# An attention layer and two quantized convolutions on one core: reading eleven images back in three pieces, and another order of products in the first two heads

## The chip, the core and the metric

The kernel runs on one core of one Trainium2 chip. A core has a matrix engine (TensorE, here PE), which multiplies a stationary operand, loaded first (PEld), by a moving one and writes to PSUM; a vector engine (DVE), a scalar engine (ACT), GpSimd (POOL) and a queue engine (SP) for DMAs. SBUF is the working memory of 128 partitions, PSUM the memory of eight banks that PE writes to. Each engine works through its own instructions in order and waits for semaphores of others. The metric is the device time of one execution in microseconds (us); lower is better.

## What is computed

The input is 16 images of 128 channels and 32 x 32 points (N = 1024). Layer 0 is attention over the points with four heads and a residual; layer 1 is two 3 x 3 convolutions on quantized activations and weights, each followed by a batch norm over all images, and a residual.

```python
qkv = einsum('bchw,oc->bohw', x, w_qkv) + b_qkv          # four heads of q, k, v
scores = einsum('bnc,bcm->bnm', q, k) * c ** -0.5
out = einsum('bnm,bmc->bnc', softmax(scores), v)
x = einsum('bchw,oc->bohw', out, w_out) + b_out + x

out = conv3x3(act_quant(x), weight_quant(w1))             # act_quant: 16 levels of [0, 1]
out = conv3x3(act_quant(batchnorm(out)), weight_quant(w2))
return batchnorm(out) + x
```

The batch norm between the convolutions needs the mean and variance of all 16 images, so the second convolution can't start before the first is done for every image.

## The kernel before

**The attention.** The weights are folded first. `fold_a(h)` makes `at_sb`, the product of the query and key weights of head h, and its bias `au_sb`; `fold_b` makes `bt_sb`, the product of value and output weights. For head number g = 4b + h (image b), `project_u(g, hf)` (L500) makes half hf of `u`, 512 of the 1024 queries: a product of `at_sb` and the image, copied out of PSUM with its bias by DVE for the very first half and by ACT otherwise. `scores(g, k)` (L545) is a step: four PSUM tiles `pss` of 128 keys x 512 queries, each followed by an exponential on ACT into one slot of `e`. A tile (c, m) has the keys of chunk k + 4c and the query half m, so it reads half m of `u` alone; the order of the four is (0, 1), (1, 1), (0, 0), (1, 0) in every step. The slots are named B12, B22, B11 and B21 in that order. DVE then combines them: T3 = B12 + B22 (L556), T1 and T2 (L557), T4 (L560). The next step's `attend` does seven half-width products of `e` and `vo` into the four banks `psa` instead of eight. A DMA of SP or GpSimd (L566, L568) adds the exponentials up for the softmax's denominator. `project_v` (L522) makes `vo` from the image and `bt_sb`, in two parts c = 0 and 1.

All of PE's products of this stage pass `product` (L402), which holds them to the order in which the program calls them. That order is written by hand: the loop at L961 runs the steps, `at(step, half, fn, ...)` puts other work behind a step's scores (half 0) or behind its `attend` (half 1), and `between` puts a call behind one tile of scores. In step 1 `between` puts the two parts of the first `project_v` behind tiles 0 and 1. The other engines' instructions are ordered by a scheduler when the program is built.

**The start.** `warm_up(3)` (L442) issues three products of a block of ones that nobody reads, into a PSUM tile of `ps_a`, while the first weights and the first image are loaded. Then come `fold_a(0)`, and both halves of `project_u(0)`, then step 0. The second head's `u` is made by `project_u(1, 0)` at (2, 1) and `project_u(1, 1)` at (3, 1) (L957, L958), the latter as the last thing before the scores of head 1. `u` and `psv` outside of the first steps share the single bank of `ps_m`.

**The first convolution** runs beside the attention, image by image. Its outputs `ys[b]` of images 4 to 14 (`AWAY`) are written to `y1d` in main memory, since SBUF is full; those of 0 to 3 and 15 stay.

**The second stage** (from L1010) reuses the SBUF of the attention. SP issues one DMA (L1046) that brings all eleven images back into `back`, and then the residual `x1` of all images (L1051). `quantize2(b)` (L1053) scales image b on ACT (L1061), clamps it on DVE (L1062) and writes it to a padded buffer, on DVE up to image 5 (L1066) and on ACT after (L1068). Six images (`FILTERED`: 3, 5, 7, 9, 11, 13) are convolved with fewer products from sums of rows, `rows` (L1077), two on DVE and two on GpSimd, and put together from the PSUM tiles `psf` by ACT (L1097) and DVE (L1098 to L1101); the others are convolved directly, `psc` (L282), and copied out by ACT (L293). DVE takes the statistics of each (L298). The loop at L1110 quantizes one image ahead: behind the convolution of image 0 image 2, of 1 image 5, of 2 image 4, of 3 image 7, of 4 image 6 and so on. Images 0 to 3 need nothing read back. When all statistics are there, each image is scaled, the residual added, and stored (L1129).

Of the kernel before, what the change touches and what calls it, by code (L numbers as in the profile page):

```python
# [9 lines left out]
F32 = mybir.dt.float32  # L10
# [183 lines left out]
def fast_path(  # L194
# [17 lines left out]
    P = 128  # L212
    B, C, N = x.shape
# [16 lines left out]
    ones = sums[:, 0 : 2 * P // (N // Q), :].rearrange("p g k -> p (g k)")  # L230
# [11 lines left out]
    AWAY = range(4, B - 1)  # L242
# [131 lines left out]
    with ExitStack() as ph:  # L374
# [27 lines left out]
        def product(out_, lhsT, rhs, start=True, stop=True):  # L402

            with tc.issue_after(pe[0]) if pe else nullcontext():
                done = nc.tensor.matmul(out_, lhsT=lhsT, rhs=rhs, start=start, stop=stop)  # L405
            pe[:] = [done.ins]
            return done
# [32 lines left out]
                nc.scalar.dma_start(out=bnp_sb, in_=bnp)  # L440

        def warm_up(n):  # L442


            ps = ps_a.tile([P, 2 * P], F32, tag="a0", name="unread")
            for _ in range(n):
                product(ps, ones[:, 0:P], ones)


        at_sb = once.tile([P, NH, P], F32, name="at_sb")  # L450
# [49 lines left out]
        def project_u(g, hf, ps=None):  # L500
            b, h = heads[g]
            if hf == 0:
                us[g] = up.tile([P, N], F32, tag="u", name=f"u_{g}")
            if ps is None:
                ps = ps_m.tile([P, HALF], F32, tag="mm", name=f"psu_{g}_{hf}")
            halves(ps, lambda t: at_sb[:, h, LANES[t]], xt[b][:, ts(hf, HALF)])
            dst = us[g][:, ts(hf, HALF)]
            if g == 0 and hf == 0:
                nc.vector.tensor_scalar(dst, ps, au_sb[:, h : h + 1], None, ALU.add)
            else:  # L510
                copied = nc.scalar.activation(dst, ps, AF.Identity, bias=au_sb[:, h : h + 1])  # L511
                if g == 0:
                    load_rest(copied.ins)
# [31 lines left out]
        def scores(g, k, between=None):  # L545


            b, h = heads[g]
            e = es[g, k] = ep.tile([P, 7, HALF], F32, tag="e", name=f"e_{g}_{k}")
            for i, (c, m) in enumerate(((0, 1), (1, 1), (0, 0), (1, 0))):  # L550
                ps = ps_s.tile([P, HALF], F32, tag="s", name=f"pss_{g}_{k}_{i}")
                score(ps, b, g, k + NK * c, ts(m, HALF))
                exps[:] = [nc.scalar.activation(e[:, 2 * c + 1 - m], ps, AF.Exp).ins]  # L553
                if between and i in between:
                    between[i]()
            nc.vector.tensor_tensor(e[:, T3], e[:, B12], e[:, B22], ALU.add)  # L556
            nc.vector.tensor_tensor(  # L557
                e[:, T1 : T2 + 1 : T2 - T1], e[:, B12 : B11 + 1], e[:, B11 : T3 + 1 : T3 - B11], ALU.subtract
            )
            last = nc.vector.tensor_tensor(e[:, T4], e[:, T2], e[:, B21], ALU.add)  # L560
            combined[g, k] = last.ins
            mine = e[:, T4 : T3 + 1]
            sums_added[:] = [last.ins]
            if k == 0:
                sides[g] = esp.tile([P, NHF, HALF], F32, tag="es", name=f"es_{g}")
                nc.sync.dma_start(out=sides[g], in_=mine)  # L566
            else:
                nc.gpsimd.dma_start(out=sides[g], in_=mine, accum_op=ALU.add)  # L568
# [336 lines left out]
        def at(step, half, fn, *args):  # L905

            later.setdefault(2 * step + half, []).append((fn, args))

        def run(step, half):
            for fn, args in later.pop(2 * step + half, ()):  # L910
                fn(*args)

        warm_up(3)
        fold_a(0)
        for hf in range(NHF):
            ps = ps_a.tile([P, HALF], F32, tag=f"a{2 + hf}", name=f"psu_0_{hf}")
            project_u(0, hf, ps)
        at(1, 0, load_second)
# [36 lines left out]
                for i, (step, half) in enumerate(when):  # L955
                    at(g * NK + step, half, project_v, b + 1, *divmod(i, 2))
        at(2, 1, project_u, 1, 0)  # L957
        at(3, 1, project_u, 1, 1)  # L958
        at(n_steps, 1, gather, 0)

        for step in range(n_steps):  # L961
            g, k = divmod(step, NK)
            between = {}
            if step == 1:
                banks = [ps_a.tile([P, HALF], F32, tag=f"a{2 + c}", name=f"psv_0_{c}") for c in range(2)]
                between = {0: lambda: project_v(0, 0, 0, banks[0]), 1: lambda: project_v(0, 0, 1, banks[1])}
            scores(g, k, between)
            if step == 0:
                fold_b()
            elif step < NK:  # L970
                project_v(0, step, 0)
            run(step, 0)
            if step > 0:
                attend(*divmod(step - 1, NK))
            if 0 < step < NK:
                ps = ps_s.tile([P, HALF], F32, tag="s", name=f"psv_0_{step}_1")
                project_v(0, step, 1, ps)
            run(step, 1)
# [31 lines left out]
    with ExitStack() as ph:  # L1010
# [31 lines left out]


        scale1, bias1 = bn_params(0)
        back = resp.tile([P, len(AWAY), N], F32, name="back")
        nc.sync.dma_start(out=back, in_=y1d.rearrange("b c n -> c b n"))  # L1046
        for i, b in enumerate(AWAY):
            ys[b] = back[:, i]
        x1 = resp.tile([P, B, N], F32, name="res")
        for some in (slice(0, B - 1), slice(B - 1, B)):  # L1050
            nc.sync.dma_start(out=x1[:, some], in_=x1d[some].rearrange("b c n -> c b n"))  # L1051
# [360 lines left out]
```

## Time and profile before

| | |
|---|---|
| time, median of 3 runs | 2020.92 us (2020.81 to 2023.84) |
| the profiled execution | 2020.84 us, of which 2018.7 us are the span of the trace |
| granted PE clock, mean | 0.992 |
| longest groups: `pss` matmuls | 1032.5 us, 4128 of them |
| `psa` matmuls | 922.4 us, 3624 of them |
| exponentials on ACT (L553) | 594.9 us, 1008 of them, 595 ns each |
| second convolution, first and last matmul | 1927.64 to 1987.3 us |
| memory traffic while the images are read back | 410 to 420 GB/s, 1921 to 1957 us |

The span is the time from the first to the last instruction; 2.1 us lie around it. A line of a group or a wait names the engine, what is written and the line of the kernel: "PE pss L405 <- ACT u L511" is PE waiting, before a product into `pss`, for ACT to write `u`. All products of the attention have line 405, that of the recording helper, so they are told apart by the tile. Matmuls overlap in the pipeline: a product of 512 columns of one pass is listed with some 590 ns and the next starts 430 ns later. PE is busy in nearly the whole span, so the places that matter are the few where it waits.

### The profile page before, as it was taken

The numbers are of one execution on the slowest core, as the hardware profiler recorded it, in microseconds if no ns is written. First come the engines' busy times: TensorE is split into PE (matmuls) and PEld (weight loads), VectorE is DVE, ScalarE is ACT, GpSimd is POOL, SyncE is SP. The second block draws the span as 40 slices with busy tenths as digits, with TensorE's granted clock in tenths as the row PEclk, the third lists the DMA queues.
The fourth block names the chain that finished last, engine by engine and source line by source line (L and its number), as shares of the span: only waits on it lengthen the run. The fifth ranks groups of instructions, "written<-read, shape, count | busy, mean of one in ns | idle before, by whom it ended". The sixth has DMA issues, their size and how long they took to land.

```text
span 2018.7 us, 25810 instructions
## 1 busy us (share of the span) xinstructions
PE 1980.5 (98%) x9676; PEld 864.9 (43%) x9677; DVE 1539.8 (76%) x2564; ACT 1185.8 (59%) x1992; POOL 187.5 (9%) x218
## 2 busy tenths in 40 slices
PE   9999999999999999999999999999999999999993
PEld 3444444444434444444444444444444444444541
DVE  3878787776878777687777868877786877778797
ACT  4565665565566566556556556655655665665575
POOL 1101000000100000010010000001001000000021
PEclk9999999999999999999999999999999999999997
DMA  3334333333433433333333333333343334324174
GB/s 85 88 71 94 74 94 73 84 74 74 94 73 84 94 75 92 75 85 83 94 84 76 92 73 94 83 94 76 71 105 74 90 78 94 84 63 97 40 292 168
DMA packets 50501, 181.19 MB, mean 90 GB/s; under 512 B 5568, under 2 KB 5952, under 8 KB 50368
## 3 DMA queue, kind: packets, MB, share of 16 engines
q0 software_dynamic: 27216, 99.10, 25.9%
q1 hardware_dynamic: 19952, 70.33, 8.9%
q10 hardware_dynamic: 3200, 10.03, 1.6%
q8 instruction: 77, 1.26, 0.3%
q14 instruction: 56, 0.46, 0.1%
HBM read 24.78 MB, written 22.54 MB: 23 GB/s over the span
## 4 chain that ended last, share of the span: by engine, by line
PE 97%; DVE 1%; issue 1%; ACT 0%; POOL 0%; DMA 0%; SPq 0%; DVEq 0%; POOLq 0%; ACTq 0%
PE pss L405 43%; PE psa L405 37%; PE psu L405 5%; PE psv L405 5%; PE psc L282 2%; PE psw L405 2%; PE psf L1086 1%; DVE back L1139 0%; POOL worst L371 0%; DVE y L1139 0%; DMA x<-in_x_dram 0%; DVE e L557 0%; ACT y L1136 0%; DVE steps L1062 0%; ACT e L553 0%
## 5 line engine op out<-in xcount | busy, mean ns | idle before, releaser
L405 PE MATMUL pss<-u,x 128*64 128x512 f32 (+1 forms) x4128 | 1032.5, 589 | 1.9 <-ACT u L511 1.6
L405 PE MATMUL psa<-e,vo 128*64 128x512 f32 (+1 forms) x3624 | 922.4, 588 | 0.0
L553 ACT ACTIVATE e<-pss 128x512 f32<-128x512 f32 x1008 | 594.9, 595 | 370.5 <-PE pss L405 366.6
L405 PEld LDWEIGHTS pss<-u,x 128*64 128x64 f32 x4128 | 391.5, 137 | 502.6 <-issue 451.2
L405 PEld LDWEIGHTS psa<-e,vo 128*64 128x64 f32 x3624 | 350.7, 137 | 428.4 <-issue 401.3
L556 DVE TENSOR_TENSOR e<-e 128x512 f32<-128x512 f32 x252 | 172.1, 683 | 352.1 <-ACT e L553 352.1
L557 DVE TENSOR_TENSOR e<-e 128x1024 f32<-128x1024 f32 x252 | 308.4, 1224 | 31.0 <-ACT e L553 20.9
L568 POOL DMA_DIRECT2D es<-e x189 | 163.0, 863 | 1688.2 <-DVE e L560 1642.8
L560 DVE TENSOR_TENSOR e<-e 128x512 f32<-128x512 f32 x252 | 174.1, 691 | 21.0
L598 ACT COPY ev<-psa 128x512 f32<-128x512 f32 x252 | 135.4, 589 | 90.2 <-PE psa L405 90.2
L405 PE MATMUL psv<-bt_sb,x 128*64 128x512 f32 x512 | 184.9, 592 | 1.0 <-ACT bt_sb L482 1.0
L405 PE MATMUL psu<-x,at_sb 128*64 128x512 f32 x512 | 184.3, 597 | 0.3 <-DMA x<-in_x_dram 0.3
L532 ACT COPY vo<-psv 128x512 f32<-128x512 f32 x128 | 75.5, 590 | 142.1 <-PE psv L405 142.1
L511 ACT ACTIVATE u<-psu,au_sb 128x512 f32<-128x512 f32 x127 | 87.3, 688 | 16.5 <-PE psu L405 14.8
L405 PEld LDWEIGHTS psv<-bt_sb,x 128*64 128x64 f32 x512 | 57.8, 137 | 65.1 <-issue 59.5
L405 PEld LDWEIGHTS psu<-x,at_sb 128*64 128x64 f32 x512 | 58.1, 138 | 63.0 <-issue 61.2
L628 DVE TRANSPOSE_TENSOR_REDUCE part<-es 128x32 f32<-128x1024 f32 (+1 forms) x65 | 79.4, 1221 | 5.9 <-DMA es<-e 5.9
L668 DVE STREAM_TRANSPOSE rb<-sums 128x1024 f32<-128x1024 f32 (+1 forms) x66 | 79.9, 1211 | 2.1
L838 ACT COPY m<-psw 128x512 f32<-128x512 f32 x45 | 26.3, 585 | 92.5 <-PE psw L405 91.4
L679 DVE TENSOR_TENSOR av<-av,rb 128x1024 f32<-128x1024 f32 x47 | 57.6, 1225 | 1.6
L680 DVE TENSOR_TENSOR acc<-acc,av 128x1024 f32<-128x1024 f32 x47 | 57.5, 1224 | 1.5
L618 ACT COPY ev<-y 64x512 f32<-64x512 f32 x63 | 38.8, 615 | 30.5 <-DVE y L616 28.6
(164 smaller groups left out, 1188.8 us busy)
## 6 DMA issues: line engine op xcount, KB each, us to landing
es<-e POOLq DMA_DIRECT2D x189, 512.0 KB, 4.5
es<-e SPq DMA_DIRECT2D x63, 512.0 KB, 2.9
x_dram<-acc SPq DMA_DIRECT2D x16, 512.0 KB, 4.4
x<-in_x_dram ACTq DMA_DIRECT2D x15, 512.0 KB, 4.7
res<-x_dram SPq DMA_DIRECT2D x1, 7680.0 KB, 35.8
y_dram<-y SPq DMA_DIRECT2D x11, 512.0 KB, 2.6
back<-y_dram SPq DMA_DIRECT2D x1, 5632.0 KB, 18.0
out_dram<-back SPq DMA_DIRECT2D x10, 512.0 KB, 3.0
```

The lines of the kernel that those rows point to most:

```text
L405: done = nc.tensor.matmul(out_, lhsT=lhsT, rhs=rhs, start=start, stop=stop)
L511: copied = nc.scalar.activation(dst, ps, AF.Identity, bias=au_sb[:, h : h + 1])
L532: nc.scalar.copy(v[:, c : c + 3 : 2], ps.rearrange("p (h a o) -> p a h o", a=2, o=PH))
L553: exps[:] = [nc.scalar.activation(e[:, 2 * c + 1 - m], ps, AF.Exp).ins]
L556: nc.vector.tensor_tensor(e[:, T3], e[:, B12], e[:, B22], ALU.add)
L557: nc.vector.tensor_tensor(e[:, T1 : T2 + 1 : T2 - T1], e[:, B12 : B11 + 1], e[:, B11 : T3 + 1 : T3 - B11], ALU.subtract)
L560: last = nc.vector.tensor_tensor(e[:, T4], e[:, T2], e[:, B21], ALU.add)
L568: nc.gpsimd.dma_start(out=sides[g], in_=mine, accum_op=ALU.add)
L598: nc.scalar.copy(to, ps)
L628: nc.vector.tensor_reduce(part, total.rearrange("p (k c) -> p k c", c=Q), AX.X, ALU.add, apply_transpose=True,)
L668: nc.vector.transpose(rb, rinv.unsqueeze(2).to_broadcast([P, n, Q]))
L679: nc.vector.tensor_tensor(av, av, rb, ALU.mult)
```

## The change

Four things are changed.

- `warm_up` writes to one tile `unread`, made once before, and one more unread product is issued before each half of `project_u(0)`.
- In the first step of the first head the tiles of query half 0 come first: (0, 0), (1, 0), (0, 1), (1, 1). All other steps stay as they are.
- In step 1 the two parts of `project_v` stand behind tiles 1 and 2 instead of 0 and 1. The second half of head 1's `u`, `project_u(1, 1)`, stands behind tile 1 of step 3's scores instead of behind that step's `attend` and the products after it.
- The eleven images come back in three DMAs into three tiles: images 4 and 5, images 6 to 8, images 9 to 14. Their sizes are 1024, 1536 and 3072 KB.

With these, the scheduler puts some instructions of ACT, DVE and SP in another order. On SP the store of the last image's residual (L762), which stood behind the single read, stands behind the first of the three. On ACT the quantizings of images 5, 4, 7 and 6 stand before copies of the second convolution's images 0 to 2 that they stood behind. On DVE, at the start, the copy of L481 stands before L560 instead of behind it.

```diff
--- before.py
+++ after.py
@@ -440,11 +440,8 @@
                 nc.scalar.dma_start(out=bnp_sb, in_=bnp)
 
         def warm_up(n):
-
-
-            ps = ps_a.tile([P, 2 * P], F32, tag="a0", name="unread")
             for _ in range(n):
-                product(ps, ones[:, 0:P], ones)
+                product(unread, ones[:, 0:P], ones)
 
 
         at_sb = once.tile([P, NH, P], F32, name="at_sb")
@@ -547,7 +544,8 @@
 
             b, h = heads[g]
             e = es[g, k] = ep.tile([P, 7, HALF], F32, tag="e", name=f"e_{g}_{k}")
-            for i, (c, m) in enumerate(((0, 1), (1, 1), (0, 0), (1, 0))):
+            tiles = ((0, 1), (1, 1), (0, 0), (1, 0))
+            for i, (c, m) in enumerate(tiles[2:] + tiles[:2] if (g, k) == (0, 0) else tiles):
                 ps = ps_s.tile([P, HALF], F32, tag="s", name=f"pss_{g}_{k}_{i}")
                 score(ps, b, g, k + NK * c, ts(m, HALF))
                 exps[:] = [nc.scalar.activation(e[:, 2 * c + 1 - m], ps, AF.Exp).ins]
@@ -910,9 +908,11 @@
             for fn, args in later.pop(2 * step + half, ()):
                 fn(*args)
 
+        unread = ps_a.tile([P, 2 * P], F32, tag="a0", name="unread")
         warm_up(3)
         fold_a(0)
         for hf in range(NHF):
+            warm_up(1)
             ps = ps_a.tile([P, HALF], F32, tag=f"a{2 + hf}", name=f"psu_0_{hf}")
             project_u(0, hf, ps)
         at(1, 0, load_second)
@@ -955,7 +955,6 @@
                 for i, (step, half) in enumerate(when):
                     at(g * NK + step, half, project_v, b + 1, *divmod(i, 2))
         at(2, 1, project_u, 1, 0)
-        at(3, 1, project_u, 1, 1)
         at(n_steps, 1, gather, 0)
 
         for step in range(n_steps):
@@ -963,7 +962,9 @@
             between = {}
             if step == 1:
                 banks = [ps_a.tile([P, HALF], F32, tag=f"a{2 + c}", name=f"psv_0_{c}") for c in range(2)]
-                between = {0: lambda: project_v(0, 0, 0, banks[0]), 1: lambda: project_v(0, 0, 1, banks[1])}
+                between = {1: lambda: project_v(0, 0, 0, banks[0]), 2: lambda: project_v(0, 0, 1, banks[1])}
+            elif step == NK - 1:
+                between = {1: lambda: project_u(1, 1)}
             scores(g, k, between)
             if step == 0:
                 fold_b()
@@ -1042,10 +1043,11 @@
 
 
         scale1, bias1 = bn_params(0)
-        back = resp.tile([P, len(AWAY), N], F32, name="back")
-        nc.sync.dma_start(out=back, in_=y1d.rearrange("b c n -> c b n"))
-        for i, b in enumerate(AWAY):
-            ys[b] = back[:, i]
+        for lo, hi in ((0, 2), (2, 5), (5, len(AWAY))):
+            back = resp.tile([P, hi - lo, N], F32, name=f"back{lo}")
+            nc.sync.dma_start(out=back, in_=y1d[lo:hi].rearrange("b c n -> c b n"))
+            for i in range(lo, hi):
+                ys[AWAY.start + i] = back[:, i - lo]
         x1 = resp.tile([P, B, N], F32, name="res")
         for some in (slice(0, B - 1), slice(B - 1, B)):
             nc.sync.dma_start(out=x1[:, some], in_=x1d[some].rearrange("b c n -> c b n"))
```

## The prediction

> **What bounds the kernel now.** I read the whole span first (busy time, then the chain that ended last), then what the matrix engine (PE) waited for, then the stretches where it waited.
>
> ```profile
> PE 1980.5 (98%) x9676; PEld 864.9 (43%) x9677; DVE 1539.8 (76%) x2564; ACT 1185.8 (59%) x1992; POOL 187.5 (9%) x218
> ...
> PE 97%; DVE 1%; issue 1%; ACT 0%; POOL 0%; DMA 0%; SPq 0%; DVEq 0%; POOLq 0%; ACTq 0%
> ```
>
> The reader sees that only time taken from PE, or a PE stall removed, can shorten the span. PE's waits, over the whole span:
>
> ```profile
> PE psc L282 <- DVE pad L1066: 2.5, 2, 2.1
> PE pss L405 <- ACT u L511: 1.6, 2, 0.8
> PE unread L405 <- POOL sums L231: 1.1, 1, 1.1
> PE psv L405 <- ACT bt_sb L482: 1.0, 1, 1.0
> PE psu L405 <- DMA x<-in_x_dram: 0.3, 1, 0.3
> PE pss L405 <- ACT e L553: 0.3, 1, 0.3
> ```
>
> (us in total, times, longest.) That is all: 6.8 us, in the first 46 us and once near 1943. The timeline of the start places the small ones:
>
> ```profile
> 5.01 2.95 PE L405 MATMUL psu<-x,at_sb 128*64 128x512 f32 x8 [0.35 <-DMA x<-in_x_dram]
> ...
> 8.74 3.65 PE L405 MATMUL pss<-u,x 128*64 128x512 f32 x16 [0.78 <-ACT u L511]
> ...
> 15.53 1.08 PE L405 MATMUL psv<-bt_sb,x 128*64 128x512 f32 x4 [1.04 <-ACT bt_sb L482]
> ...
> 45.41 3.65 PE L405 MATMUL pss<-u,x 128*64 128x512 f32 x16 [0.79 <-ACT u L511]
> ```
>
> The chain of waits around the big one (start, us, what), and then the busy time of the engines there (columns: us, busy and count of PE, PEld, DVE, ACT, POOL, then granted clock, DMA share, GB/s):
>
> ```profile
> 1938.32 1.25 ACT steps L1061
> ...
> 1940.52 1.73 DVE rows L1077 x2
> 1942.24 1.27 DVE steps L1062
> ...
> 1944.51 5.79 PE psc L282 x18
> ...
> 1952.94 3.97 PE psc L282 x18
> ```
>
> ```profile
> 1938.00:1944.00 6.00, 4.37 (x20) 1.75 (x18) 5.03 (x7) 5.91 (x7) 2.67 (x2) 1.00 1.03 419
> 1944.00:1950.00 6.00, 5.49 (x18) 2.17 (x19) 6.00 (x11) 3.76 (x4) 2.48 (x2) 0.72 1.03 410
> 1950.00:1956.00 6.00, 6.00 (x29) 2.65 (x28) 5.99 (x12) 5.68 (x8) 1.03 (x1) 1.00 1.02 409
> ```
>
> Image 4 comes back from memory, ACT can first quantize from it at 1938.32, and PE's convolution of image 4 starts at 1944.51 after 2.14 us idle. Its 18 matmuls then take 5.79 us where the next 18 take 3.97: the clock share is 0.72 in that stretch. So one late read costs 2.14 + (5.79 - 3.97) = about 3.9 us. From 1944 on DVE is busy 6.00 and 5.99 of 6 us, so it is nearly as tight as PE.
>
> ```profile
> back<-y_dram SPq DMA_DIRECT2D x1, 5632.0 KB, 18.0
> ```
>
> ```profile
> L1077 DVE TENSOR_TENSOR rows<-padf x12: 428/1074/1367, 1931.5 to 1970.6; 128x544 bf16<-128x544 bf16 x12
> ```
>
> The read of 5632 KB lands after 18.0 us, at 1937.3; ACT's first use is 1 us later.
>
> **What the Trainium skill says.** "TensorE: Matmul & The Clock Gate", section "What's actually happening": PE falls to half clock after an idle window of 3413 ns, the window runs freely. The trace agrees with the length: (1 - 0.72) x 6 us = 1.7 us lost, so 3.4 us at half; here 2.1 us idle were enough. "DMA: Bandwidth & Descriptors", "Queues, rings and completion order": descriptors are consumed in ring order. The trace agrees: the 512 KB store of the last image, issued behind the big read, needs 17.1 us to land (median of such stores 4.4), so a small first piece will land early. "SBUF — State Buffer", "SBUF: two separate sides": DVE operations with two SBUF inputs or in a two-port mode and GpSimd operations exclude each other. It agrees: the same subtraction on DVE takes 428 to 1367 ns, the long ones beside GpSimd's.
>
> **The change part by part.**
>
> *Part A, the start.* Two unread products are added, one before each half of `psu`. At the half clock of this point one costs two passes of 0.43 us (passes start at 1.68, 2.10, 2.53 in the trace). The first starts at about 4.45, when the bias product is issued; it fills the 0.35 us idle and pushes `psu` 0 from 5.01 to about 5.30. `psu` 0 takes 2 x 0.87, the second unread product goes in at 7.04, by then at full clock (passes of 0.21): `psu` 1 at 7.49, done issuing at 8.35. The scores no longer wait for ACT's second half of `u`: the two tiles put first read only the half that DVE wrote (0.75 us, here 7.26 to 8.01). So scores start at 8.35 instead of 8.74: 0.39 us gained. But all four exponentials now come before DVE's first combination, since B12 and B22 are last: the last exponential ends at 12.65, then 0.69 (L556) and 1.23 (L557) on DVE, ready 14.65. The scheduler puts the copy L481 before L560 in exchange, so it ends at 14.85; L560, 0.69, and the subtraction L483, 0.43, at 15.80. `psv` waits for it and for ACT's L482, which now stands behind a second exponential: that one starts at 15.00 (13.88 for its scores plus the 1.12 us that exp follows them by), L482 at 15.49 plus 0.45. `psv` starts at 16.0. It started at 15.53 with one tile of scores (0.86 us) still to do; that tile is now done before it. So 15.53 + 0.86 - 16.0 = 0.4 us gained, and PE's idle before it grows from 1.04 to about 1.25. Bounds: -0.2 if the cold clock lasts over both unread products (then 1.7 us of them, less the idle they fill and the 1.2 us no longer waited), +0.8 if `psv` comes earlier than I work out.
>
> *Part B, head 1.* `psu` 1 moves from 43.54, right ahead of the scores that wait for it, to between the second and third tile of step 3 (near 36.0). The 0.79 us wait at 45.41 goes. What is late next: the bank of `psu` 0, which ACT frees at 36.03, so at most 0.06 us there; the next user of that bank (`psv` of step 3) comes 1.7 us after `psu` 1, ACT's copy ends 0.95 us after it at the latest. Gain 0.75, bounds 0.5 to 0.8.
>
> *Part C, the reading back.* One DMA becomes three of 1024, 1536 and 3072 KB: two more issues on SP (0.38 us each, nobody waits for SP there). The first keeps all waits of the single one, the last of which is the end of the attention matmuls at 1919.2, so nothing starts earlier. The store of the last image is next in SP's queue, then the other two pieces. At 412 GB/s from 1921: the first piece lands near 1924, the second (3.15 MB in all) near 1929 to 1931, the third where the store landed before, 1938.6. ACT's order is changed with it: image 5 is quantized behind image 2, at 1931.6, image 4 at 1933.2, images 7 and 6 at 1934.8, and the third piece is first wanted near 1943. No read is waited for. Image 4 is in its padded buffer at about 1940.1: DVE's `rows` of image 5 beside GpSimd's to 1938.3, then 0.41, 0.68, 0.41 and 0.43. PE wants it at 1942.4. So the 2.14 us and the 1.8 us of slow clock go: 3.9 as the upper bound. But DVE becomes the limit. It was idle only 0.46 + 1.34 + 0.45 us before 1944, and 0.7 in small steps from 1960. Following DVE in its new order with the durations of the trace, it waits about 1.7 us for ACT near 1941 to 1944 (ACT now does five 1.2 us quantizings ahead of the copies of image 2), and is then only about 1 us ahead of before; from there to the end it saves the blocked passes (0.44 instead of 1.07 to 1.37) where GpSimd has long finished its part of `rows`, about two of them. I get the last statistics at 1985.0 against 1987.84, PE alone 1984.0. Gain 2.9; bounds 1.2 (no blocked pass saved) and 3.9.
>
> The middle has no PE wait at all, so A and B shift all of it; the end from 1990 is ACT, DVE and stores, unchanged, and the residual's read (landed at 1957.7, wanted at 1990) stays covered. **Sum:** 0.4 + 0.75 + 2.9 = 4.05 us. The profiled execution took 2020.84 us (span 2018.7 and 2.1 around it): 2016.8. The median of the runs shown is 2020.92, 0.08 above, so I take 2016.8 as it is.
>
> **Rivals.** *DVE keeps up* (for it: it has 0.56 us of slack at the last statistics and fewer blocked passes; against: 6.00 of 6 us busy): C is 3.9, sum 5.05, 2015.8. *DVE saves nothing but its idle time* (for it: every `rows` still meets GpSimd; against: their starts move apart): C is 1.2, sum 2.35, 2018.5. *The pieces don't do what they are for*, because ACT waits for another piece or the stall only moves to image 6 (for it: ACT is busy 5.91 of 6 us at 1938): C is 0, 2019.7. *Slower:* DVE and ACT, with more work put early, fall behind so that PE finds its PSUM banks or padded images unready at two of the later filtered images (5 to 13). Each such stall of 2 us costs what the one of now costs, 3.9 us, with the clock drop; one undoes C, two make it 2020.84 - 1.15 + 3.9 = 2023.6. It decides from about 2 us idle in one place; for it speaks the full DVE, against it that eight banks hold about 6 us of products and PE never waited after 1950.
>
> **How the numbers follow.** Forecast 0.45 (own range 2016.0 to 2017.7), DVE keeps up 0.25, DVE saves nothing 0.15, pieces don't help 0.07, slower 0.08. About 0.2%, 4.0 us, is what a measurement of this kernel can tell from no change: 2016.88. The forecast lies on that line, a little over half of it below: faster 0.26 + 0.25 = 0.51; slower 0.07; the rest, 0.42, within. Range 2015.2 to 2019.3: from below the first rival, with the bound of A, to the bound between the second and third.
>
> **What would show it.** Right: PE's waits list no `pss` on `u`, one `psv` on `bt_sb` or L483 of about 1.2 us; scores start near 8.35; no PE gap over 1 us after 1926, clock 1.00 there; first piece landing in about 5 us. Wrong: a PE wait for `pad` left, DVE idle after 1944, the clock at half until after 10 us, or a new wait in 4 to 50 us.

## The result, and the profile after

| | before | changed |
|---|---|---|
| time, median of 8 runs each, side by side | 2021.2 us (2019.9 to 2024.36) | 2015.62 us (2014.63 to 2017.3) |
| the profiled execution | 2020.84 us, span 2018.7 | 2016.69 us, span 2014.2 |

The ratio of the times is 0.997, with a 95% interval of 0.996 to 0.9981. Against 2020.92 us that is 2014.9 us, 2012.8 to 2017.1. The forecast of 2016.8 us hits the changed kernel's profiled execution (2016.69), and the interval still holds it, but the median lies 1.2 us below it and the ratio's centre lies under the low end of the range, 2015.2. So the kernel gains more than was worked out, and the question is where.

First the whole span of the changed kernel, busy times and the shares of the chain:

```profile
PE 1979.3 (98%) x9681; PEld 867.4 (43%) x9681; DVE 1537.1 (76%) x2564; ACT 1185.6 (59%) x1992; POOL 187.2 (9%) x218
...
PE 94%; DVE 3%; issue 1%; ACT 1%; POOL 0%; DVEq 0%; POOLq 0%; ACTq 0%
```

PE is still nearly the whole chain, with 1.2 us less of busy time although it issues two more unread products: eight of image 4's 18 products had run at half clock, 0.43 us apart instead of 0.22, and none does now. DVE's share of the chain has grown from 1% to 3%: in the second convolution the chain now runs along DVE, which is hardly ever idle there (53.8 of 56.5 us busy). That does not make it the limit; the run with fewer statistics, below, tests it. What PE waits for, in us in total, times and longest:

```profile
PE unread L405 <- POOL sums L231: 1.1, 1, 1.1
PE psv L405 <- ACT bt_sb L479: 1.0, 1, 1.0
PE psc L282 <- DVE pad L1068: 0.3, 1, 0.3
PE pss L405 <- ACT e L551: 0.3, 1, 0.3
```

Gone are both waits of `pss` for `u` (1.6 us), the 0.3 us of `psu` for the image, and, of the two waits of `psc` for `pad`, the one of 2.1 us. What is left is 2.7 us of 6.8. The timeline of PE at the start and at head 1 (start, us, what, idle time before it in brackets):

```profile
4.52 1.20 PE L405 MATMUL unread<-sums 128*128 128x256 f32 x2
5.65 1.30 PE L405 MATMUL psu<-x,at_sb 128*64 128x512 f32 x4
6.88 0.70 PE L405 MATMUL unread<-sums 128*128 128x256 f32 x2
7.51 1.08 PE L405 MATMUL psu<-x,at_sb 128*64 128x512 f32 x4
8.42 3.60 PE L405 MATMUL pss<-u,x 128*64 128x512 f32 x16
...
16.02 1.08 PE L405 MATMUL psv<-bt_sb,x 128*64 128x512 f32 x4 [1.04 <-ACT bt_sb L479]
...
44.13 3.65 PE L405 MATMUL pss<-u,x 128*64 128x512 f32 x16
```

The scores start without a wait, at 8.42 us, but `psv` still has its 1.04 us. Head 1's scores follow the products before them directly. The same stretches of the second stage as before (us, busy and count of PE, PEld, DVE, ACT, POOL, then granted clock, DMA share, GB/s):

```profile
1938.00:1944.00 6.00, 6.00 (x28) 2.63 (x27) 4.25 (x9) 5.58 (x7) 2.22 (x2) 1.00 1.03 412
1944.00:1950.00 6.00, 6.00 (x29) 2.67 (x28) 6.00 (x12) 6.00 (x8) 2.16 (x2) 1.00 1.02 406
1950.00:1956.00 6.00, 6.00 (x29) 2.68 (x28) 6.00 (x13) 5.59 (x7) 1.61 (x3) 1.00 1.02 404
```

PE has 6.00 of 6 us in each, at a clock of 1.00, where it had 4.37, and then 5.49 at 0.72. The image that was late, 4, is convolved from 1940.92 us on, straight behind the products before it. The three reads, from issue to landing in us:

```profile
back<-y_dram SPq DMA_DIRECT2D x1, 3072.0 KB, 16.4
back<-y_dram SPq DMA_DIRECT2D x1, 1536.0 KB, 8.2
back<-y_dram SPq DMA_DIRECT2D x1, 1024.0 KB, 4.8
```

SP issued them between 1918.1 and 1921.1 us, so the last landed near 1937.5, as late as the single read, while images 4 and 5 were there about 14 us sooner. And the row sums (ns shortest/median/longest, first and last start):

```profile
L1079 POOL TENSOR_TENSOR rows<-padf x12: 1128/1132/1327, 1930.0 to 1962.1; 128x544 bf16<-128x544 bf16 x12
L1079 DVE TENSOR_TENSOR rows<-padf x12: 423/428/1365, 1930.2 to 1965.9; 128x544 bf16<-128x544 bf16 x12
```

DVE's median is 428 ns where it was 1074: most passes no longer meet GpSimd's.

Three sections account for the two profiled executions. From the first product into `psa` to the first of head 1 into `ps_bo` ("head 1" from here on): 28.26 us before, 27.34 after. From the first product of the second convolution to the end of the last instruction on its statistics, L325 ("the stage"): 60.45 and 56.49. The start, up to the first product into `psa`: 20.73 and 20.37. The middle between them is 1878.65 and 1878.64 us long. With 30.57 and 31.40 us from the last statistics to the end of the span, the sum is 0.36 + 0.92 + 3.96 - 0.83 = 4.41 us of the 4.42 between the spans.

### The profile page after: what moved, and what is told of

Same layout as the page of the kernel before. It is cut to its first block, busy times and chain, and to the rows that moved or that the text cites. A ratio compares the mean times of both kernels' runs of the same rounds, so it can differ in the third digit from the quotient of the medians.

```text
span 2014.2 us, 25821 instructions
## 1 busy us (share of the span) xinstructions
PE 1979.3 (98%) x9681; PEld 867.4 (43%) x9681; DVE 1537.1 (76%) x2564; ACT 1185.6 (59%) x1992; POOL 187.2 (9%) x218
## 4 chain that ended last, share of the span: by engine, by line
PE 94%; DVE 3%; issue 1%; ACT 1%; POOL 0%; DVEq 0%; POOLq 0%; ACTq 0%
PE pss L405 43%; PE psa L405 37%; PE psv L405 5%; PE psu L405 5%; PE psw L405 2%; DVE early L298 1%; DVE back L1141 0%; DVE rows L1079 0%; POOL worst L371 0%; PE unread L405 0%; DVE steps L1064 0%; PE psc L282 0%; DVE total L1100 0%; DVE half L1102 0%; DVE y L1141 0%
```

## The experiments

All traces in one table, to be referred to below. "Full clock" is where the trace's record of the granted clock first has it full. The three sections are in us. The ratio is to the kernel before on the same chip, whose median was 2021.2 us beside the changed kernel, 2020.95 beside the next four runs, 2021.01 beside the four after them, then 2021.62 beside two and 2020.66 beside the last two.

| run | full clock at | first `psa` | head 1 | stage | time, median | ratio, 95% interval |
|---|---|---|---|---|---|---|
| before | 7.09 | 20.73 | 28.26 | 60.45 | | |
| changed | 6.14 | 20.37 | 27.34 | 56.49 | 2015.62 | 0.997, 0.996 to 0.9981 |
| pieces alone | 5.71 | 20.14 | 28.26 | 56.49 | 2016.93 | 0.9983, 0.9974 to 0.9991 |
| start alone | 6.87 | 20.73 | 28.25 | 60.46 | 2020.41 | 0.9996, 0.9987 to 1.0004 |
| head 1 alone | 4.09 | 19.98 | 27.35 | 60.45 | 2019.97 | 0.9996, 0.9987 to 1.0004 |
| changed, no added unread | 4.32 | 19.94 | 27.34 | 56.49 | 2015.14 | 0.9972, 0.9961 to 0.9984 |
| before, wait filled | 4.78 | 20.56 | 28.26 | 59.27 | 2019.64 | 0.9999, 0.9991 to 1.0008 |
| changed, fewer statistics | 5.82 | 20.21 | 27.34 | 56.49 | 2015.68 | 0.9976, 0.9967 to 0.9985 |
| changed, rows on DVE | 6.80 | 20.69 | 27.35 | 57.01 | 2015.73 | 0.9974, 0.9965 to 0.9983 |
| changed, two pieces | 5.80 | 20.23 | 27.35 | 56.49 | 2016.13 | 0.998, 0.9972 to 0.9988 |
| start and head 1 | 4.53 | 20.02 | 27.35 | 60.45 | 2019.45 | 0.9988, 0.9982 to 0.9995 |
| values later, no added unread | 8.85 | 19.86 | 27.35 | 56.49 | 2015.12 | 0.9963, 0.9949 to 0.9977 |
| changed, again | 7.17 | 20.88 | 27.35 | 56.48 | 2016.03 | 0.9974, 0.9965 to 0.9984 |
| values later | 5.09 | 19.04 | 27.35 | 56.49 | 2014.6 | 0.9969, 0.9957 to 0.9981 |

The times of the kernel before vary by some 5 us from execution to execution (2018.75 to 2024.91 in one set of 25), but head 1 and the stage repeat to 0.01 us in every trace that has the same code there. So a change is measured best in its own section, and the times tell whether the sections add up.

The spread of the times itself changes with the start. Eight sets of executions have the old order of the start: the five of the kernel before, the pieces alone, head 1 alone and the wait filled. Of their 160 executions 24 lie more than 2 us above the median of their set. Of the 105 executions in the ten sets with the new order one does. The standard deviations are 1.2 to 1.9 us in the old sets and 0.4 to 1.1 in the new. The two sets with the new order and no added unread products are narrow too, so the narrowing does not need those products; the order of tiles and the place of `project_v` are what those sets have of the start. None of the long executions was traced, so what takes longer in them is not shown.

**The pieces alone.** The kernel before with nothing but the three reads:

```diff
-        back = resp.tile([P, len(AWAY), N], F32, name="back")
-        nc.sync.dma_start(out=back, in_=y1d.rearrange("b c n -> c b n"))
...
+        for lo, hi in ((0, 2), (2, 5), (5, len(AWAY))):
+            back = resp.tile([P, hi - lo, N], F32, name=f"back{lo}")
+            nc.sync.dma_start(out=back, in_=y1d[lo:hi].rearrange("b c n -> c b n"))
...
```

> Only the eleven images are read back in three pieces. Theory 1 (the whole cost of the late read goes: 2.14 us of stall and 1.8 us of slow clock, and DVE keeps up): 3.9 us faster than before, ratio 0.998; no PE wait of 2 us near 1943, full clock to the end of the convolutions. Theory 2 (DVE limits the stage, and the rest of the measured gain comes from the start): 2.9 us faster at most, PE with small waits for banks after 1950.

The stage, in the columns used above:

```profile
1927.25:1983.74 56.49, 55.73 (x270) 26.10 (x270) 53.80 (x101) 41.28 (x54) 13.89 (x12) 1.00 0.54 216
```

It takes 56.49 us, 3.96 less than with one read, and the median is 4.0 us lower. That is all of what the late read cost (2.14 + 1.82), not the 2.9 us of the forecast. Theory 1 holds.

**The start alone.** The unread products, the order of tiles in step 0 and `project_v` one tile later, nothing else:

```diff
...
+            warm_up(1)
             ps = ps_a.tile([P, HALF], F32, tag=f"a{2 + hf}", name=f"psu_0_{hf}")
...
-                between = {0: lambda: project_v(0, 0, 0, banks[0]), 1: lambda: project_v(0, 0, 1, banks[1])}
+                between = {1: lambda: project_v(0, 0, 0, banks[0]), 2: lambda: project_v(0, 0, 1, banks[1])}
```

> Only the start: unread products, the order of the first four tiles, psv one tile later. Theory 1: 0.4 us faster, psa starts at 20.4 instead of 20.7. Theory 2: about 2 us faster in the timed executions, since there the clock stays low for longer in the kernel before than its profile shows; and a smaller spread of times.

The first product into `psa` is at 20.73 us, where it was before, and the time can't be told from before. Of theory 2 the smaller spread came (a standard deviation of 0.95 us against 1.59 of the kernel before beside it), the 2 us did not. PE's waits show what was removed and what was not: the wait of `psu` for the image and the first one for `u` are gone, head 1's wait for `u` and the late image are there.

```profile
PE psc L282 <- DVE pad L1067: 2.5, 2, 2.1
...
PE psv L405 <- ACT bt_sb L480: 1.0, 1, 1.0
PE pss L405 <- ACT u L509: 0.8, 1, 0.8
```

**Head 1 alone.** `project_u(1, 1)` between the tiles of step 3, nothing else:

```diff
-        at(3, 1, project_u, 1, 1)
...
+            if step == NK - 1:
+                between = {1: lambda: project_u(1, 1)}
```

> Only the second half of head 1's u is moved into step 3. Both theories: the wait of 0.79 us before head 1's scores goes, 0.8 us faster, a ratio of 0.9996.

Head 1 takes 27.35 us instead of 28.26. On the timeline the four products of `psu` no longer stand between `ps_a` and the scores, and the 0.79 us wait is gone:

```profile
43.21 0.61 PE L405 MATMUL ps_a<-wqk_sb 128*128 128x128 f32 x4
43.74 3.65 PE L405 MATMUL pss<-u,x 128*64 128x512 f32 x16
```

So 0.91 us come from here, 0.12 more than the wait itself.

**The changed kernel without its two added unread products.**

```diff
-            warm_up(1)
             ps = ps_a.tile([P, HALF], F32, tag=f"a{2 + hf}", name=f"psu_0_{hf}")
```

> The changed kernel without the two unread products. Theory 1: they only fill 0.35 us and cost 1 us of PE that the order of the tiles hides, so 0 to 0.6 us faster than the changed kernel in its profile, 5.0 to 6.0 us faster than before. Theory 2: the clock comes later without them, so about 1 us slower than the changed kernel and with a larger spread.

Nothing is lost without them: 2015.14 us, the stage and head 1 as in the changed kernel. In its trace full clock came at 4.32 us, sooner than in any trace with them. The larger spread of theory 2 did not come either: the standard deviation is 0.42 us.

**The wait filled.** The kernel before, with ten unread products in front of image 4's convolution:

```diff
+        if n == 1 and b == 4 and r == 0:
+            for _ in range(10):
+                nc.tensor.matmul(
...
+                    rhs=wq[0].rearrange("p t o -> p (t o)")[:, 0:HALF],
...
```

> The kernel before, with ten unread products of 512 columns put into the matrix engine's wait for image 4 (they write the bank that the convolution of image 4 then overwrites). The single late read stays. Ten take 2.2 us at full clock, about what the wait lasted (2.14 us). Theory 1 (the late read costs two things, the wait and a stretch at half clock that the wait brings on): the wait of about 2.1 us stays, now filled, the granted clock stays at 1.00 between 1944 and 1950 us, the 18 products of image 4 take about 4.0 us instead of 5.79, so from the first product of the second convolution to the last statistics it takes 60.45 - 1.8 = about 58.6 us, and the time falls by about 1.8 us, to 2019.2. Theory 2 (the clock falls for another reason, or the lost clock is hidden behind the vector engine, which is busy all the time from 1944 us on): the stage keeps its 60.4 us within 0.3 and the time stays at 2020.9.

The timeline has the unread products in the place of the wait, and image 4's 18 products at 4.0 us (the next start less this one) instead of 5.79. The clock stays at 1.00 in the stretches below it:

```profile
1941.69 2.32 PE L282 MATMUL psc<-wq 128*128 128x512 bf16 x10
1944.00 4.13 PE L291 MATMUL psc<-pad,wq 128*128 128x512 bf16 x18
1947.97 1.48 PE L1095 MATMUL psf<-rows,middle 128*128 128x512 bf16 x6
```

The busy times and the clock of the same kernel there:

```profile
1938.00:1944.00 6.00, 6.00 (x28) 2.58 (x27) 5.49 (x9) 5.40 (x6) 2.67 (x2) 1.00 1.02 418
1944.00:1950.00 6.00, 6.00 (x29) 2.67 (x28) 6.00 (x10) 5.03 (x6) 2.48 (x2) 1.00 1.02 409
```

So the half clock does come from the wait: with the array kept at work in it, it doesn't happen. PE starts its last product 57.76 us after the stage's first, where it was 59.43: 1.67 us. But the stage shrinks by 1.18 us only (60.45 to 59.27), not by the expected 1.8: DVE goes through the last seven passes of statistics without a gap, where in the kernel before it waited 0.28 us for ACT and 0.56 us for PE among them. Here, with the single read, DVE does limit. The time does not decide: the median is 1.4 us lower, but the ratio's interval includes no change.

**Fewer statistics.** The changed kernel, less work on DVE (the statistics of four images are left out, and the buffer for them is set to zero once):

```diff
...
-            if b < B - 1:
+            if b < B - 1 and b not in (5, 7, 9, 11):
                 done = statistics(b, 1)
```

> The changed kernel without the second convolution's statistics of images 5, 7, 9 and 11 (their mean and variance are left out of the batch norm): eight passes of 0.68 us, 5.4 us, are taken from the vector engine in the stage that it was thought to limit; the matrix engine's work is the same. Theory 1 (the matrix engine alone sets the stage, the vector engine keeps up): the matrix engine's last product and the last statistics stay where they are, 56.5 us after the first product of the stage, within 0.2 us, and the time stays at 2015.6 within 0.5. Theory 2 (the vector engine limits the stage by about 1 us, as the prediction had it): the stage shrinks to 55.5 us and the time to about 2014.6.

The stage takes 56.49 us, to the hundredth what it takes with all statistics, although DVE has 48.6 us of work in it instead of 53.8. On DVE's timeline it waits for PE's last products:

```profile
1980.06 1.02 DVE L293 BATCH_NORM_STATS2 late<-psc 128x6 f32<-128x512 f32 x2
1981.63 0.43 DVE L293 BATCH_NORM_STATS2 late<-psc 128x6 f32<-128x256 f32 x1 [0.55 <-PE psc L283]
```

In the changed kernel the same three passes stand nearly without a gap (0.09 us, for PE, before the last), and end at the same distance from the stage's start:

```profile
1981.01 1.54 DVE L292 BATCH_NORM_STATS2 late<-psc 128x6 f32<-128x512 f32 x3
1982.59 0.25 DVE L325 BATCH_NORM_AGGREGATE mv<-late 128x2 f32<-128x21 f32 x1
```

So in the changed kernel PE sets the stage, and DVE arrives with it, with 0.09 us of slack left. The forecast had DVE 1 us behind.

**All row sums on DVE.** The changed kernel, no `rows` on GpSimd:

```diff
-                engine = nc.vector if k in (1, 2) else nc.gpsimd
+                engine = nc.vector
```

> The changed kernel with all four row sums of each filtered image on the vector engine, none on GpSimd. Twelve more passes of 0.43 us, 5.2 us, go to the vector engine; what it loses beside GpSimd's passes in the changed kernel, about 5.1 us over twelve passes, should go. Theory 1 (the long passes come from GpSimd working at the same time, and the vector engine has room): every pass takes 0.42 to 0.44 us, the vector engine's busy time between 1936 and 1984 us stays the same within 0.5 us, and the stage stays at 56.5 us. Theory 2 (the long passes have another cause, such as memory traffic at 410 GB/s): passes above 1 us remain, the vector engine gets about 5 us more work than it has room for, the matrix engine waits, and the stage grows by 2 us or more.

The row sums of this kernel (ns shortest/median/longest, first and last start):

```profile
L1079 DVE TENSOR_TENSOR rows<-padf x24: 425/432/442, 1930.5 to 1965.6; 128x544 bf16<-128x544 bf16 x24
```

Not one pass is long any more, under the same 410 GB/s of memory traffic. So the long ones come from GpSimd, and DVE does all 24 in 10.4 us of busy time; in the kernel before twelve took 11.4. DVE's busy time in the stage is 52.8 us, 1 us less than in the changed kernel rather than the same within 0.5. It does not help the time: PE waits once for an image that ACT writes (L1070), 0.36 us, and the stage is 0.5 us longer. Why that image is later was not followed up.

**Two pieces.** Images 4 and 5, and all the others:

```diff
-        for lo, hi in ((0, 2), (2, 5), (5, len(AWAY))):
+        for lo, hi in ((0, 2), (2, len(AWAY))):
```

> The changed kernel with two pieces instead of three: images 4 and 5 (1024 KB), then images 6 to 14 (4608 KB). Images 6 to 8 then land near 1938.6 us instead of 1931. Theory 1 (only image 4 was late, so only the first piece has to be small): the scalar engine is given image 7 about 5 us later, but the matrix engine wants it at 1944.9 us and gets it in time; no wait of the matrix engine, stage 56.5 us, time 2015.6. Theory 2 (the second cut is needed as well): the scalar engine stands still at images 7 and 6 with copies of finished products behind it, or image 7's padded buffer is late; the matrix engine waits 1 to 3 us near 1940 to 1946, with or without a half clock behind it, and the stage takes 57.5 to 60.5 us, the time 2016.6 to 2019.6.

The two reads of this kernel, from issue to landing in us:

```profile
back<-y_dram SPq DMA_DIRECT2D x1, 4608.0 KB, 16.7
back<-y_dram SPq DMA_DIRECT2D x1, 1024.0 KB, 4.9
```

The scalar engine gets images 7 and 6 at 1938.61 and 1940.23 us instead of from 1933.51 on, and PE waits for none of them: the stage is 56.49 us. Only the first cut is needed. DVE is worse off with it (55.1 us busy, `rows` as long as before the change), and has 1.4 us of idle time left in the whole stage: the second cut buys DVE room, which PE doesn't need here.

**Start and head 1 without the pieces.** The changed kernel with the single read put back (the diff of the first experiment, reversed).

> The changed kernel with the single read put back, so with the start and head 1 alone: the complement of the run with the three pieces alone. Theory 1 (the three parts act apart from each other, and the pieces carry the whole of the stage): the stage takes 60.4 to 60.5 us with the wait of 2.1 us and 3.41 us at half clock in it, head 1 gains 0.9, the start 0 to 0.4, and the time is 1.0 to 1.5 us below the kernel before, 2019.5 to 2020.0. Theory 2 (the start and head 1 together carry a good part of the gain, about 2 us): 2018.5 to 2019.

Its two stretches around the late image (columns as before):

```profile
1938.00:1944.00 6.00, 3.86 (x17) 1.43 (x16) 5.64 (x9) 4.61 (x6) 2.67 (x2) 0.94 1.02 416
1944.00:1950.00 6.00, 6.00 (x23) 2.44 (x22) 5.97 (x10) 4.05 (x5) 2.48 (x2) 0.77 1.03 412
```

The late image and the half clock are back (3.41 us of it, from 1943.30), the stage is 60.45. The median is 2.2 us below before, the ratio's 1.2 parts in a thousand are 2.4 us (1.0 to 3.6 by its interval): the size that theory 2 named. The sections say otherwise: the stage gives nothing, head 1 its 0.91 us, and the start, 20.02 against 20.73 us, 0.71 us in an execution whose clock was full 2.6 us sooner, and the old order does as well with such a clock (19.98 us in the trace with head 1 alone). So theory 1 has the stage and head 1. The rest of the time's difference, about 1 us, is in no section. It goes with the narrower spread (the slowest of the 25 executions of before took 2024.91 us, the slowest of these 21 took 2021.1), but what it is was not traced.

**The values later.** The remaining 1.04 us wait of `psv`: the parts of `project_v` go behind tiles 2 and 3. First without the added unread products, then with them and beside the changed kernel itself, on one chip:

```diff
-                between = {1: lambda: project_v(0, 0, 0, banks[0]), 2: lambda: project_v(0, 0, 1, banks[1])}
+                between = {2: lambda: project_v(0, 0, 0, banks[0]), 3: lambda: project_v(0, 0, 1, banks[1])}
```

> The changed kernel without the two unread products, and with the two parts of the first value product behind tiles 2 and 3 of step 1 instead of 1 and 2. The matrix engine waits 1.04 us there for the copy L479. Theory 1 (one more tile of scores, 0.86 us, fills the wait): the wait falls to about 0.2 us, the first product into psa starts at 19.1 to 19.3 us after the same start where it was at 19.94, and the time is about 0.8 us below that of the kernel without the unread products, 2014.3. Theory 2 (what is behind the value product is late instead: the values go through copies and a sum before psa can use them, 1.3 us after the last product): a new wait of 0.7 to 1.3 us ahead of psa takes the place of the one removed, and the time stays at 2015.1 within 0.4.

> The changed kernel itself once more, beside the next run on the same chip. Theory 1: the stage takes 56.5 us, head 1 27.3 us from the first product into psa to head 1's next weights, and the first product into psa comes at 20.2 to 20.7 us, depending on when the clock becomes full; 5.2 to 5.6 us below the kernel before. Theory 2 (the first profile of it was a lucky one and the stage's gain varies): the stage takes over 57 us here.

> The changed kernel with its unread products, and the two parts of the first value product behind tiles 2 and 3 of step 1. Theory 1 (the wait of 1.04 us is filled and nothing behind it is late): the wait falls to about 0.2 us and the first product into psa comes about 0.8 us earlier than in the run beside it if the clock becomes full at the same time, the time is 0.5 to 0.9 us below that of the changed kernel. Theory 2 (what the clock does in the first 9 us decides, not the wait): the two times agree within 0.4 us.

The changed kernel's second trace repeats the stage (56.48 us) and head 1 (27.35), as theory 1 has it; the first product into `psa` comes at 20.88 us, a little past the 20.2 to 20.7 expected, and the time is 4.6 us below before on that chip, a little less than 5.2 to 5.6. In both runs with the values later the wait falls to 0.18 us and none comes in its place. On PE's timeline of the last one:

```profile
12.58 2.79 PE L405 MATMUL pss<-u,x 128*64 128x512 f32 x12
15.56 1.08 PE L405 MATMUL psv<-bt_sb,x 128*64 128x512 f32 x4 [0.18 <-ACT bt_sb L479]
16.47 1.03 PE L405 MATMUL pss<-u,x 128*64 128x512 f32 x4
17.32 1.89 PE L405 MATMUL psv<-bt_sb,x 128*64 128x512 f32 x8
19.04 3.17 PE L405 MATMUL psa<-e,vo 128*64 128x512 f32 x13
```

`psa` starts at 19.04 us; starts of the changed order with full clock at 4.53 and 5.80 us had it at 20.02 and 20.23. Without the added unread products it came at 19.86 although the clock was full only at 8.85 us. The medians are 2014.6 with them, against 2016.03 for the changed kernel beside it, and 2015.12 without. The two ratios of the last pair, 0.9969 and 0.9974, have intervals that overlap widely, but both carry the spread of the kernel before. Set directly beside each other, all six executions with the values later (2014.1 to 2014.99) lie below nine of the ten of the changed kernel (2014.91 to 2017.03). So on this chip it is faster, by 1.4 us in the medians, where 0.5 to 0.9 was expected; 0.86 us of it is the wait.

## Why the prediction was right and where it was not

**The step that failed is in Part C: "But DVE becomes the limit", "Gain 2.9".** The first half of the part was right in every link: the first piece landed in 4.8 us, ACT quantized images 5, 4, 7 at 1930.27, 1931.87 and 1933.51, which are the predicted times less the 1.3 us by which the whole stage had moved up; the wait and the slow clock went. What was wrong is DVE's time in the new order, which was put 1 us too long. The forecast's 2.9 us were about 1 us that DVE is ahead once it has waited for ACT, and after that "about two" long passes, 0.63 to 0.93 us each. What came instead is in the busy times over the whole stage, of the kernel before, the changed one and the one with two pieces (columns as above):

```profile
1927.64:1988.09 60.45, 57.55 (x270) 26.45 (x270) 56.30 (x101) 41.80 (x54) 14.67 (x12) 0.97 0.50 200
1926.35:1982.84 56.49, 55.73 (x270) 26.12 (x270) 53.80 (x101) 41.23 (x54) 13.90 (x12) 1.00 0.54 217
1926.01:1982.50 56.49, 55.73 (x270) 26.11 (x270) 55.07 (x101) 41.17 (x54) 14.42 (x12) 1.00 0.54 217
```

DVE has the same 101 instructions in each. From before to changed its busy time falls by 2.50 us and its idle time, the rest of the stage, from 4.15 to 2.69, by 1.46. Together that is 3.96 us, where the forecast's path of DVE had 2.9. Two terms of it were short.

- Idle: the waits for ACT were sized well (1.7 us forecast; 0.48 + 0.83 + 0.45 = 1.76 between 1939.6 and 1942.7). But before, DVE also waited 0.28 us for ACT and 0.56 for PE among its last passes. The forecast names the 0.56 us under its rivals and does not use it in its sum. In the changed kernel 0.09 us of these is left.
- Busy: before, eight of the twelve passes of `rows` were long (0.77 to 1.37 us), five of them among the last eight. After, the first four are long and the last eight, from the third filtered image on, all take 0.42 to 0.43 us: `rows` went from 11.4 to 8.3 us and lost 3.1, of which 1.0 came back as longer clamps (`steps`, L1064, 7.42 to 8.42 us).

The two pieces show that the long passes alone don't decide: there DVE's busy time falls by 1.23 us only, but its idle time falls to 1.42, and the stage is the same. So C was 3.96 and not 2.9: the rival "DVE keeps up", which had chance 0.25, is what happened. The run with fewer statistics shows it (5.2 us taken off DVE, 53.8 to 48.6, move the end by nothing), and the pieces alone show it without the rest. How near it was, the filled wait shows: with DVE in its old order, 0.5 us of what PE gained was lost to DVE.

**"The Trainium skill", "SBUF — State Buffer", section "SBUF: two separate sides".** The exclusion of DVE and GpSimd was the right thing to reckon with, and the run with all rows on DVE agrees with it: 24 passes of 425 to 442 ns with GpSimd idle, up to 1365 beside it. But such passes can't be carried from one order into another by counting: in the changed kernel GpSimd's two passes for the third filtered image ended at 1943.45 us and DVE's first began at 1944.25, where before they overlapped. The forecast let about two go where among the last eight all five went, while two clamps more than before became long (0.85 and 0.99 us instead of 0.42).

**Part B: 0.75 predicted, 0.92 measured** (28.26 to 27.34 us, 27.34 or 27.35 in all ten traces with the move). The mechanism was right. The term that was too small is the wait's own 0.79 us, less the 0.06 us at the bank of `psu` 0, of which nothing is seen; and 0.13 more is saved than the wait. In the kernel before, the products ahead of that wait are these:

```profile
43.54 1.08 PE L405 MATMUL psu<-x,at_sb 128*64 128x512 f32 x4
```

The wait of 0.79 us is counted from their listed end, 44.62. But where nothing is waited for, the next product starts some 0.86 us after the first of four such (16.47 to 17.32 in the last timeline above). So PE lost about 1.0 us there, from 44.40 to 45.41, and 0.92 of it was gained.

**Part A: 0.4 predicted; nothing at the same clock.** In the two profiled executions the start is 0.36 us shorter, and 8.42 and 16.02 us for scores and `psv` are within 0.1 of the predicted 8.35 and 16.0. That is agreement by chance: the clock was full at 6.14 us in one and at 7.09 in the other. Sorted by that moment, the start ends at 19.98, 20.14 and 20.73 us in the old order (full clock at 4.09, 5.71, 7.09), and at 20.02, 20.23, 20.21, 20.37, 20.69, 20.73 and 20.88 in the new (4.53, 5.80, 5.82, 6.14, 6.80, 6.87, 7.17). The two rows lie on one curve within about 0.15 us. (The filled wait has the old order and is off it, 20.56 at 4.78: there PE waited 0.7 us for the image.) From the first score to `psa` it is 11.99 us before and 11.95 after, so what follows the scores changes as little as predicted; the step that failed is "pushes `psu` 0 from 5.01 to about 5.30", the price of the unread products. The timeline has `psu` 0 at 5.65: the first unread product took 1.13 us, not 0.85, and the second 0.63 (6.88 to 7.51), not 0.45. In that execution the clock made up for it, as it became full within `psu` 0, which took 1.23 us instead of 1.74. The changed kernel's second trace has the clock that the sum assumes, full at 7.17 us:

```profile
5.66 1.81 PE L405 MATMUL psu<-x,at_sb 128*64 128x512 f32 x4
7.40 0.70 PE L405 MATMUL unread<-sums 128*128 128x256 f32 x2
8.03 1.08 PE L405 MATMUL psu<-x,at_sb 128*64 128x512 f32 x4
8.94 3.60 PE L405 MATMUL pss<-u,x 128*64 128x512 f32 x16
```

Here `psu` 0 takes its 1.74 us, the second unread product 0.63 again, and the scores start at 8.94, later than the 8.74 of before at 7.09. Without the two products nothing is won either (19.94 us at 4.32); there `psu` 1 waits 1.06 us for the image instead. The start alone gave a ratio of 0.9996, which can't be told from no change. What the start does change is the spread of the times, told below the table, of which Part A says nothing.

**The sum.** 3.96 + 0.92 + 0 is 4.9 us, and the medians say 5.58 the first time and 4.63 the second. The forecast's 4.05 lacked 1.06 in C and 0.17 in B and had 0.4 too much in A. The sections alone, taken from 2020.84, would give 2015.9 us, which is inside the range of the forecast; that the ratio's centre is 2014.9 needs about 1 us more, which is in no section. It may be the narrower spread; that is not shown. That its 2016.8 us agrees with the one profiled execution (2016.69) is again chance: the end behind the last statistics, which the forecast took as unchanged, took 0.83 us longer in it than in the profiled execution of before. Over all traces that end is anywhere from 30.49 to 31.48 us.

**Of the signs listed:** no `pss` waits for `u`, `psv` has one wait on L479, the scores start near 8.35, no gap of PE over 1 us after 1926 and a clock of 1.00: all seen. Of the signs against, "a PE wait for `pad` left" is there with 0.3 us, at the first product of the stage. It is not new: the 2.5 us of the kernel before were two waits, and the shorter, 0.34 us at 1927.64, was left out of "once near 1943". "DVE idle after 1944" did not come in the changed kernel, as DVE was just in time; it came in the run with fewer statistics.

## What to carry to other kernels

A transfer that is needed piece by piece should be cut so that the first piece holds what is wanted first: here 1 MB of 5.5 in front was enough, and the stage got back not only the 2.1 us of waiting but nearly as much again, 1.8 us, of slow clock. When the engine next in line is predicted to limit, work out its time with the contention at its least and at its most, since which passes meet changed with the order here. And measure a section between two marks of the trace as well as the whole: two sections repeated to 0.01 us where whole executions varied by 5. But the sections of a few traces don't show what a change does to the spread of the times, which needs many executions.

## What was not expected of the hardware

- The moment of full clock at the start varies more than anything the change does there. It was first recorded anywhere from 4.09 to 8.85 us in fourteen traces: 4.53 to 7.17 in the eight with the added unread products, 4.09 to 8.85 in the six without them. "TensorE: Matmul & The Clock Gate", section "What's actually happening", says that the window runs freely and that the moment varies with it; the spread here is larger than the half microsecond to either side that it gives (it also reports one kernel with 6, 11 or 14 products at half clock).
- One wait of 2.1 us, less than the window of 3413 ns that the prediction takes from the same section, was enough to bring a half-clock stretch of 3.41 us in every trace with the single read and nothing in the wait (four of four). The stretch began 0.05 to 1.35 us after the wait's end. Ten unread products in the wait prevented it.
